# A graph network on one core: degrees written transposed and the scaled adjacency stored graph by graph

## The chip, the cores and the metric

The kernel runs on one core of a Trainium2 chip, in fp32 throughout. The metric is the device time of one execution in microseconds (us), as the median of three runs. A profiled execution is a fourth one; its trace gives the durations that are used below.

## The reference

There are 128 graphs with 128 nodes each and 512 features per node. Two residual layers follow each other, each closed by a layer norm over the features:

```python
# layer 0
deg = jnp.sum(adj, axis=-1, keepdims=True)
agg = jnp.einsum('bij,bjf->bif', adj, x) / jnp.maximum(deg, EPS)
cat = jnp.concatenate([x, agg], axis=2)
out = jnp.einsum('bnf,of->bno', cat, W)          # W: 512 x 1024
x = _layernorm(x + jax.nn.relu(out))
# layer 1: three times adj @ (x @ W_k) + b_k, relu after the first two
support = jnp.einsum('bnf,fh->bnh', x, W)
return jnp.einsum('bnm,bmh->bnh', adj, support) + b
...
x = _layernorm(x + layer_1)
```

What matters here is the division by the degree: the row of the adjacency that belongs to node i of a graph is divided by that row's sum.

## The kernel before, in words

The graphs are worked on in 32 groups of four, called quads (`NG` = 32, `G` = 4), numbered q = 0 to 31 in the code; "the sixth quad" is q = 5. All products run on TensorE. The large weight products use a seven-product scheme for blocks of two by two; after the first one or two quads it is nested, and then the operand of one such product is a 128x128 block (line 617) where the first quads use 128x256 (line 599). Prepared combinations of the first layer's weights lie in DRAM (`forms`) and are streamed into buffers named `ring` and `big`.

The division by the degree is done on the adjacency, not on the result. For a quad this goes through these steps:

- `load_adj` (line 543) loads the adjacency rows into `ar`, of which there is one buffer (every DMA of the kernel is recorded by a helper at line 320).
- `degrees` (line 550) sums each row on VectorE (line 554, `deg<-ar`), takes the maximum with a small number (line 555) and the reciprocal (line 556). The result `deg` is a tile of 128 partitions by 4: partition i holds the factors of node i of the four graphs. There are two `deg` buffers.
- One DMA writes `deg` to `dd` in DRAM (two buffers), with 16 bytes in a row for each node. A second DMA reads all 512 numbers of `dd` back into every one of the 128 partitions of `ah` (one buffer).
- `normalized` (line 563) multiplies `ah` by the transposed adjacency `at` on VectorE (line 327, `ah<-at,ah`). The order of the 512 numbers in a partition of `ah` is node first, graph second: the factors of one graph stand four floats, that is 16 bytes, apart. `at` is stored graph by graph.
- `seg_agg` (line 907) runs, for each graph g, a matmul with `AH_T[:, :, g]` as the weights (the operand that is loaded into the array ahead of the product) and 512 columns of `row` as the moving operand (line 916). In fp32 each such matmul becomes two weight loads and two passes in the trace, so that the four graphs of a quad give eight of each.

The order of the work is made in two steps. A list written out by hand (`ORDER`, `AFTER`) says in which order the stages of the quads are recorded; stage `D` is the loading of the adjacency and its degrees. Then a planner (`Plan.order`) replays all recorded operations with its own costs, its due times and the dependencies through named buffers, and emits each engine's instructions in the order in which the replay started them. It may give a GpSimd addition to VectorE (`other`) when it is late. An engine then works through its instructions strictly in that order, and SyncE's DMA queue as well: a DMA whose buffer isn't free holds back every DMA behind it. The buffer names that order `degrees` are `ar`, `deg`, `dd` and `ah`: a write to `dd` waits until the read of the same buffer into `ah` has landed.

Of the kernel before, what the change touches and what calls it, by code (L numbers as in the profile page):

```python
# [9 lines left out]
F32 = mybir.dt.float32  # L10
AF = mybir.ActivationFunctionType
OP = mybir.AluOpType
AX = mybir.AxisListType

P = 128
G = 4
# [227 lines left out]
def gnn_resnorm_kernel(  # L244
# [15 lines left out]
    nc = tc.nc  # L260
# [6 lines left out]
    dram = ctx.enter_context(tc.tile_pool(name="dram", bufs=1, space=bass.MemoryType.DRAM))  # L267
# [6 lines left out]
    def tile_of(shape, name):  # L274
        return sbuf.tile(shape, F32, tag=name, name=name)
# [8 lines left out]
    U_T = [tile_of([P, 4, 2, H], f"u{i}") for i in range(2)]  # L284
    AR_T = tile_of([P, G, P], "ar")
    AT_T = [tile_of([P, G, P], f"at{i}") for i in range(2)]
    AH_T = tile_of([P, P, G], "ah")
    ND = 8
    DEG_T = [tile_of([P, G], f"deg{i}") for i in range(2)]
    DD_T = [dram.tile([P, G], F32, tag=f"dd{i}", name=f"dd{i}") for i in range(2)]  # L290
    FORMS = dram.tile([7, P, 7, 2, P], F32, tag="forms", name="forms")
    ST_T = [tile_of([P, 6], f"st{i}") for i in range(ND)]
    END_ST = tile_of([P, 2, 2, 6], "end_st")
# [15 lines left out]
    def pinned(ins):  # L309
        return tc.keep_in_program_order(ins)  # L310

    def vector(n, emit, reads, writes, shared=False, lead=None):
        plan.op("DVE", 0.06 + 0.00123 * n, emit, reads, writes, shared, lead=lead)

    def scalar(n, emit, reads, writes, columns=0, lead=None):
        plan.op("ACT", 0.165 + 0.00083 * n + 0.1 * columns, emit, reads, writes, lead=lead)

    def dma(dst, src, reads, writes, size, queue="SP", lead=None):
        eng = nc.sync if queue == "SP" else nc.scalar
        plan.op(queue, 0.06, lambda: pinned(eng.dma_start(dst(), src())), reads, writes, size=size, lead=lead)  # L320

    def const(v):
        return lambda: v

    def add(eng, n, dst, a, b, reads, writes, op=OP.add, shared=False, lead=None):

        on_vector = lambda: pinned(nc.vector.tensor_tensor(dst(), a(), b(), op=op))  # L327
        if eng == "POOL":
            on_gpsimd = lambda: pinned(nc.gpsimd.tensor_tensor(dst(), a(), b(), op=op))  # L329
            plan.op("POOL", 0.03 + 0.00243 * n, on_gpsimd, reads, writes, True, other=(0.06 + 0.00123 * n, on_vector), lead=lead)  # L330
        else:
            vector(n, on_vector, reads, writes, shared)
# [195 lines left out]
    def at(q):  # L528
        return AT_T[q % 2], [("at", q % 2)]
# [16 lines left out]
    def load_adj_t(q):  # L546
        t, k = at(q)
        dma(const(t), const(adjT[q]), (), k, P * F * 4)

    def degrees(q):  # L550
        d, kd = DEG_T[q % 2], [("deg", q % 2)]
        dd = DD_T[q % 2]
        queue = "ACT" if q == 0 else "SP"
        vector(512, lambda: pinned(nc.vector.tensor_reduce(d, AR_T, axis=AX.X, op=OP.add)), ["ar"], kd)
        vector(90, lambda: pinned(nc.vector.tensor_scalar(d, d, DEG_EPS, None, op0=OP.max)), kd, kd, True)
        vector(90, lambda: pinned(nc.vector.reciprocal(d, d)), kd, kd)
        dma(const(dd), const(d), kd, [("dd", q % 2)], 400000 if q else 800000, queue)
        dma(
            const(AH_T), const(bass.AP(tensor=dd.tensor, offset=dd.offset, ap=[[0, P], [G, P], [1, G]])),
            [("dd", q % 2)], ["ah", "row of degrees"], 400000, queue,  # L560
        )

    def normalized(q):
        t, k = at(q)
        ah = AH_T.rearrange("p i g -> p g i")
        add("DVE", 512, const(ah), const(t), const(ah), k + ["ah"], ["ah"], OP.mult, True)

    def bank_ap(s):
        return BANK[s.index]
# [253 lines left out]
    def layernorm(i, ap, keys, of=None):  # L823

        i %= ND
        mv, rs = MV_T[i], RS_T[i]
        src, ksrc = of or (ap, keys)
        for j in range(2):
            st = ST_T[(2 * i + j) % ND]
            ks = [("st", (2 * i + j) % ND)]  # L830
            vector(512, lambda j=j, st=st: pinned(nc.vector.bn_stats(st, src(j))), ksrc(j), ks)
            vector(98, lambda j=j, st=st: pinned(nc.vector.bn_aggr(mv[:, j, :], st)), ks, [("mv", i, j)])
        kr, kb = factors(i, range(2))
        for j in range(2):
            r, b = rs[:, 0, j : j + 1], rs[:, 1, j : j + 1]
            scalar(
                512,
                lambda j=j, r=r, b=b: pinned(nc.scalar.activation(ap(j), src(j), AF.Identity, bias=b, scale=r)),
                kr + kb + ksrc(j), keys(j), columns=2,
            )  # L840
# [51 lines left out]
    def l0(q):  # L892
        return row(q, "y"), u_of(q)

    def seg_l0(q, part):
        y, u = l0(q)
        if part == 0:
            normalized(q)
        if q < EARLY:
            name, w, t = ("y", WB, y) if part < 2 else ("l0", WA, u)  # L900
            yield from (rows_b if part % 2 else rows_a)((name, q), xa(q), w, t)
        elif part < 2:
            yield from joint_a(q, xa(q), WBA, (y, u), part)
        else:
            yield from joint_b(q, xa(q), WBA, (y, u), part - 2)

    def seg_agg(q, m):
        y, u = l0(q)
        for g in (2 * m, 2 * m + 1):
            p, r = Slot("bank", seeded=True), Slot("s", spare=3)  # L910
            dma(lambda r=r: S_T[r.index].rearrange("p a b -> p (a b)"), const(x[q][:, g]), (), [r], P * F * 4, lead=LEADS[1])
            scalar(512, lambda g=g, p=p: pinned(nc.scalar.copy(bank_ap(p), u.graph(g))), u.keys((g,)), [p], lead=LEADS[0])
            plan.op(
                "PE", 0.858,
                lambda g=g, p=p: pinned(
                    nc.tensor.matmul(bank_ap(p), AH_T[:, :, g], y.graph(g), start=False, stop=True, skip_group_check=True)  # L916
                ),
                ["ah"] + y.keys((g,)), [p],
            )
            vector(  # L920
                512,
                lambda g=g, p=p, r=r: pinned(
                    nc.vector.scalar_tensor_tensor(
                        u.graph(g), bank_ap(p), 0.0, S_T[r.index], op0=OP.max, op1=OP.add
                    )
                ),
                [p, r], u.keys((g,)),
            )
            yield
        layernorm(4 * q + m, lambda j: u.graph(2 * m + j), lambda j: u.keys((2 * m + j,)))  # L930
# [317 lines left out]
    WB.sums()  # L1248
    load_adj(0)
    degrees(0)  # L1250
    load_adj_t(0)
    WA = Weight("wa", w0T[0:F])
# [21 lines left out]
    def load_degrees(q):  # L1274
        load_adj(q)
        degrees(q)
        yield

    def load_at(q):
# [4 lines left out]
        "X": load_x, "D": load_degrees, "AT": load_at,  # L1284
        **{f"L{i}": lambda q, i=i: seg_l0(q, i) for i in range(4)},
        **{f"A{i}": lambda q, i=i: seg_agg(q, i) for i in range(2)},
        **{f"G{i}": lambda q, i=i: seg_g1(q, i) for i in range(4)},
        "Ha": seg_h1_a, "Hb": seg_h1_b, "Sa": seg_s2_a, "Sb": seg_s2_b, "H2": seg_h2, "Ta": seg_s3_a, "Tb": seg_s3_b,
# [48 lines left out]
    for t in range(NG + max((lag for _, lag in tokens), default=0)):  # L1337
        for n, lag in tokens:
            q = t - lag
# [57 lines left out]
```

## Time and profile before

| | before |
|---|---|
| median of three runs | 2249.04 us (2248.91 to 2249.4) |
| the profiled execution's own time | 2250.41 us |
| its span, from the first to the last instruction | 2248.5 us |
| TensorE (PE) busy | 2235.7 us, 13,624 passes and as many weight loads |
| VectorE (DVE) busy | 1534.5 us |
| ScalarE (ACT) busy | 1330.8 us |
| GpSimd (POOL) busy | 1168.4 us |
| granted TensorE clock | 0.999 |
| DMA packets | 206,330 |
| one quad in the steady state | 69.4 us of PE |

The span of the profiled execution is 1.9 us shorter than its time, and its time is 1.4 us above the median of the timed runs. In the profile a group of instructions has its line, engine, operation, the names of what it writes and reads without buffer numbers, its shape and its count; behind the bar stand the busy time in us and the mean duration of one in ns. "PE" rows are passes of matmuls, "PEld" rows are weight loads, which run while the pass before them is still streaming. Durations of pipelined passes overlap, so a busy PE row is less than count times mean.

### The profile page before, as it was taken

How to read it: one execution, taken by the hardware profiler on the slowest of the kernel's cores; microseconds unless marked ns; L12 is line 12 of the kernel's file. 1: busy time of each engine (PE TensorE's matmuls, PEld its weight loads, DVE VectorE, ACT ScalarE, POOL GpSimd, SP SyncE). 2: the span in 40 equal slices, each digit the busy share in tenths (PEclk: the TensorE clock that was granted, in tenths of full speed). 3: DMA queues.
4: the chain of work that ended last, by engine and by line, in shares of the span. 5: the costliest groups of instructions: out<-in, count | busy, mean ns of one | idle time of the engine just before them, and what ended most of it. 6: DMA issues, size and time to landing. Idle time of an engine off the chain costs nothing.

```text
span 2248.5 us, 39986 instructions
## 1 busy us (share of the span) xinstructions
PE 2235.7 (99%) x13624; PEld 1997.9 (89%) x13624; DVE 1534.5 (68%) x3384; ACT 1330.8 (59%) x2619; POOL 1168.4 (52%) x1508
## 2 busy tenths in 40 slices
PE   8999999999999999999999999999999999999998
PEld 7888889898898888998888989889898898888997
DVE  4766667666777667677666766667666777667674
ACT  2456656566565665566665656656566556665565
POOL 0245654556645465554565455654546655455540
PEclk9999999999999999999999999999999999999999
DMA  8453445534455444454444553445534455443431
GB/s 268 125 156 125 149 142 174 175 121 145 130 176 176 127 146 134 159 176 140 139 144 143 178 162 124 147 142 172 176 121 149 129 168 176 124 141 129 153 125 38
DMA packets 206330, 333.14 MB, mean 148 GB/s; under 512 B 27056, under 2 KB 72112, under 8 KB 206128
## 3 DMA queue, kind: packets, MB, share of 16 engines
q1 hardware_dynamic: 205696, 330.19, 46.1%
q8 instruction: 109, 1.79, 0.3%
q14 instruction: 93, 0.76, 0.1%
q10 hardware_dynamic: 432, 0.40, 0.1%
HBM read 290.46 MB, written 40.04 MB: 147 GB/s over the span
## 4 chain that ended last, share of the span: by engine, by line
PE 99%; DVE 0%; DMA 0%; issue 0%; SPq 0%; DVEq 0%; ACT 0%
PE bank L617 57%; PE bank L599 21%; PE bank L916 5%; PE bank L941 5%; PE bank L1029 5%; PE bank L1216 5%; DMA big<-in_w0T_dram 0%; DVE big L327 0%; PE bank L1148 0%; SPq L320 0%; DVE ah L327 0%; DVE end_st L1153 0%; DVEq L1392 0%; DVE bank L327 0%; DVE T L327 0%
## 5 line engine op out<-in xcount | busy, mean ns | idle before, releaser
L579 ACT COPY s<-bank 128x384 f32<-128x384 f32 (+1 forms) x567 | 306.6, 541 | 320.6 <-PE bank L617 172.3
L599 PE MATMUL bank<-T,w 128*128 128x256 f32 x1792 | 416.9, 379 | 0.0
L599 PEld LDWEIGHTS bank<-T,w 128*128 128x128 f32 x1792 | 333.5, 190 | 67.2 <-issue 28.7
L329 POOL TENSOR_TENSOR T<-T 128x512 f32<-128x512 f32 (+2 forms) x295 | 279.8, 971 | 199.6 <-DVE T L327 113.2
L327 DVE TENSOR_TENSOR v<-bank,s 128x512 f32<-128x512 f32 x240 | 164.3, 684 | 205.1 <-PE bank L617 204.3
L617 PE MATMUL bank<-big,ti 128*128 128x128 f32 (+1 forms) x1470 | 274.2, 320 | 0.0
L329 POOL TENSOR_TENSOR xT<-xT 128x512 f32<-128x512 f32 (+1 forms) x244 | 237.9, 975 | 36.0 <-DVE ti L327 23.6
L585 ACT COPY bank<-bank 128x512 f32<-128x512 f32 (+2 forms) x273 | 144.0, 527 | 180.0 <-PE bank L617 153.4
L617 PEld LDWEIGHTS bank<-big,ti 128*128 128x128 f32 x1470 | 218.4, 191 | 23.8 <-issue 4.3
L617 PEld LDWEIGHTS bank<-w,T 128*128 128x128 f32 x1680 | 218.3, 192 | 17.1 <-issue 7.2
L327 DVE TENSOR_TENSOR T<-T 128x512 f32<-128x512 f32 (+1 forms) x325 | 223.9, 713 | 8.8 <-ACT T L952 5.8
L617 PEld LDWEIGHTS bank<-w,ti 128*128 128x128 f32 x1680 | 216.1, 192 | 15.5 <-issue 7.2
L617 PE MATMUL bank<-w,T 128*128 128x128 f32 x1680 | 226.5, 275 | 0.0
L617 PE MATMUL bank<-w,ti 128*128 128x128 f32 x1680 | 226.5, 275 | 0.0
L617 PE MATMUL bank<-big,T 128*128 128x128 f32 x1680 | 226.4, 275 | 0.0
L617 PEld LDWEIGHTS bank<-big,T 128*128 128x128 f32 x1680 | 218.3, 192 | 7.7
L327 DVE TENSOR_TENSOR row<-bank,s 128x384 f32<-128x384 f32 (+2 forms) x254 | 119.0, 468 | 152.3 <-PE bank L617 124.8
L617 PE MATMUL bank<-ring,xT 128*128 128x256 f32 x840 | 216.7, 380 | 0.0
L617 PE MATMUL bank<-big,xT 128*128 128x256 f32 x840 | 216.7, 379 | 0.0
L329 POOL TENSOR_TENSOR v<-v 128x384 f32<-128x384 f32 (+1 forms) x61 | 69.3, 1136 | 278.9 <-DVE v L327 144.4
L327 DVE TENSOR_TENSOR v<-v 128x512 f32<-128x512 f32 (+1 forms) x299 | 190.7, 645 | 5.3 <-DVE T L327 0.3
L329 POOL TENSOR_TENSOR s<-s,v 128x256 f32<-128x256 f32 (+1 forms) x60 | 51.8, 863 | 255.2 <-ACT bank L1210 140.7
(99 smaller groups left out, 4166.1 us busy)
## 6 DMA issues: line engine op xcount, KB each, us to landing
big<-forms SPq DMA_DIRECT2D x315, 256.0 KB, 3.2
ring<-forms SPq DMA_DIRECT2D x315, 256.0 KB, 3.3
s<-in_x_dram SPq DMA_DIRECT2D x128, 256.0 KB, 5.9
out_dram<-s SPq DMA_DIRECT2D x126, 256.0 KB, 4.0
xT<-in_xT_dram SPq DMA_DIRECT2D x62, 512.0 KB, 5.6
big<-forms SPq DMA_DIRECT2D x105, 128.0 KB, 2.7
ring<-forms SPq DMA_DIRECT2D x105, 128.0 KB, 2.8
ar<-in_adj_dram SPq DMA_DIRECT2D x32, 256.0 KB, 2.6
```

Source lines behind the costliest of these rows:

```text
L327: on_vector = lambda: pinned(nc.vector.tensor_tensor(dst(), a(), b(), op=op))
L329: on_gpsimd = lambda: pinned(nc.gpsimd.tensor_tensor(dst(), a(), b(), op=op))
L579: scalar(n * P, lambda: pinned(nc.scalar.copy(quarters_of(s, n), quarters(p, n))), [p], [s])
L585: scalar(n * P, lambda: pinned(nc.scalar.copy(quarters(s, n), quarters(p, n))), [p], [s])
L599: nc.tensor.matmul(bank_ap(p)[:, o, :], lhsT, rhs, start=start and o == 0 and c == 0, stop=c == 1, skip_group_check=True,)
L617: nc.tensor.matmul(dst, ta(), tb(), start=start and n == 0, stop=True, skip_group_check=True)
L916: nc.tensor.matmul(bank_ap(p), AH_T[:, :, g], y.graph(g), start=False, stop=True, skip_group_check=True)
L941: nc.tensor.matmul(bank_ap(p)[:, c // 2, (c % 2) * P : (c % 2 + 1) * P], u.chunk(g, c), a[:, g, :], start=c == 0, stop=True, skip_group_ch ...
L1029: nc.tensor.matmul(bank_ap(p)[:, g // 2, (g % 2) * P : (g % 2 + 1) * P], s.chunk(g, o), a[:, g, :], start=g == 0, stop=True, skip_group_ch ...
L1216: nc.tensor.matmul(bank_ap(p), a[:, g, :], s.graph(g), start=False, stop=True, skip_group_check=True)
```

## The change

From the sixth quad on (`by_graph`), the factors are written to DRAM graph by graph: the element of node i and graph g goes to place g*128 + i instead of i*4 + g. Neighbours in a partition of `deg` are then no neighbours in `dd`, and the write consists of single 4-byte pieces. The read into every partition of `ah` takes the 512 numbers in the order in which they lie, as before, so `ah` is now stored graph by graph, and both the multiplication with `at` and the weight operand of line 916 (`ah(q)[:, g]`) run over neighbouring floats. The first five quads keep the old order. `deg` and `dd` get four buffers each instead of two, in all quads.

```diff
-    AH_T = tile_of([P, P, G], "ah")
+    AH_T = tile_of([P, G * P], "ah")
     ND = 8
-    DEG_T = [tile_of([P, G], f"deg{i}") for i in range(2)]
-    DD_T = [dram.tile([P, G], F32, tag=f"dd{i}", name=f"dd{i}") for i in range(2)]
+    DEG_T = [tile_of([P, G], f"deg{i}") for i in range(4)]
+    DD_T = [dram.tile([G * P], F32, tag=f"dd{i}", name=f"dd{i}") for i in range(4)]
...
+    def by_graph(q):
+        return q >= 5
+
     def degrees(q):
-        d, kd = DEG_T[q % 2], [("deg", q % 2)]
-        dd = DD_T[q % 2]
+        d, kd = DEG_T[q % 4], [("deg", q % 4)]
+        dd = DD_T[q % 4]
...
-        dma(const(dd), const(d), kd, [("dd", q % 2)], 400000 if q else 800000, queue)
+        to = dd.rearrange("(g i) -> i g", g=G) if by_graph(q) else dd.rearrange("(i g) -> i g", g=G)
+        dma(const(to), const(d), kd, [("dd", q % 4)], 400000 if q else 800000, queue)
         dma(
-            const(AH_T), const(bass.AP(tensor=dd.tensor, offset=dd.offset, ap=[[0, P], [G, P], [1, G]])),
-            [("dd", q % 2)], ["ah", "row of degrees"], 400000, queue,
+            const(AH_T), const(bass.AP(tensor=dd.tensor, offset=dd.offset, ap=[[0, P], [1, G * P]])),
+            [("dd", q % 4)], ["ah", "row of degrees"], 400000, queue,
         )
+
+    def ah(q):
+        return AH_T.rearrange("p (g i) -> p g i" if by_graph(q) else "p (i g) -> p g i", g=G)
 
     def normalized(q):
         t, k = at(q)
-        ah = AH_T.rearrange("p i g -> p g i")
-        add("DVE", 512, const(ah), const(t), const(ah), k + ["ah"], ["ah"], OP.mult, True)
+        add("DVE", 512, const(ah(q)), const(t), const(ah(q)), k + ["ah"], ["ah"], OP.mult, True)
...
-                    nc.tensor.matmul(bank_ap(p), AH_T[:, :, g], y.graph(g), start=False, stop=True, skip_group_check=True)
+                    nc.tensor.matmul(bank_ap(p), ah(q)[:, g], y.graph(g), start=False, stop=True, skip_group_check=True)
```

## The prediction

> **What bounds the kernel now.** I read the page's busy times and chain first, then the waits of TensorE, then its groups with shapes apart, and last its timeline around one quad.
>
> ```profile
> PE 2235.7 (99%) x13624; PEld 1997.9 (89%) x13624; DVE 1534.5 (68%) x3384; ACT 1330.8 (59%) x2619; POOL 1168.4 (52%) x1508
> ...
> PE 99%; DVE 0%; DMA 0%; issue 0%; SPq 0%; DVEq 0%; ACT 0%
> ```
>
> These are busy time, share of the span and instructions of each engine, and the chain that ended last: TensorE (PE) is busy all the time and the chain never leaves it. Its waits (us in total, times, longest) say the same:
>
> ```profile
> PE bank L599 <- DMA big<-in_w0T_dram: 5.5, 1, 5.5
> PE bank L599 <- DVE T L327: 0.8, 1, 0.8
> PE bank L916 <- DVE ah L327: 0.2, 1, 0.2
> ```
>
> 6.5 us in total, all of it in the first quads. So a microsecond taken from any other engine is worth nothing, and the change can gain only where TensorE's own passes are longer than they need be. The groups of line 916 (weights `ah`) and of line 1216 (the same shape, weights `at`) show such a place:
>
> ```profile
> L916 PE MATMUL bank<-row,ah 128*128 128x512 f32 x256 | 128.2, 622 | 0.2 <-DVE ah L327 0.2
> L1216 PE MATMUL bank<-row,at 128*128 128x512 f32 x252 | 123.4, 592 | 0.0
> ...
> L916 PEld LDWEIGHTS bank<-row,ah 128*128 128x128 f32 x256 | 74.2, 314 | 15.7 <-DVE ah L327 0.6
> ...
> L1216 PEld LDWEIGHTS bank<-row,at 128*128 128x128 f32 x252 | 47.7, 190 | 20.1 <-issue 15.3
> ```
>
> A weight load from `ah`, whose floats stand 16 bytes apart, takes 314 ns where one from `at`, whose floats are neighbours, takes 190. The passes of line 916 are 30 ns longer in the mean. The timeline of TensorE for one quad shows which of them:
>
> ```profile
> 720.67 0.94 PE L617 MATMUL bank<-w,T 128*128 128x128 f32 x7
> 721.45 2.86 PE L916 MATMUL bank<-row,ah 128*128 128x512 f32 x6
> 724.14 1.05 PE L617 MATMUL bank<-w,ti 128*128 128x128 f32 x8
> 725.04 1.06 PE L617 MATMUL bank<-big,ti 128*128 128x128 f32 x8
> 725.93 1.14 PE L916 MATMUL bank<-row,ah 128*128 128x512 f32 x2
> 726.91 0.50 PE L617 MATMUL bank<-w,T 128*128 128x128 f32 x3
> ```
>
> The columns are start and length in us. Line 916 runs in two groups, of six passes and of two, each behind 128-column passes. The trace's starts give a step of 429 ns from one 512-column pass to the next and 112 ns from one 128-column pass to the next. A 314-ns load hides behind a 512-column pass and doesn't hide behind a 128-column one. The second group shows it alone: 726.91 - 725.93 = 0.98 us for two passes, where 2 x 0.429 = 0.858; 0.12 is over. In the first, 724.14 - 721.45 = 2.69 against 6 x 0.429 = 2.574; again 0.12. The first pass of a group lasts 712 ns and all others 592.
>
> [...] The trace has such a transfer, the loads of two bias vectors in 4-byte pieces; the landings are below.
>
> **The change part by part.** In the built program the order of the change's TensorE instructions is that of before, but for two matmuls moved behind three others in an early quad. So I price each part against an unchanged order.
>
> *Weights stored graph by graph.* 27 quads (q = 5 to 31) have two groups each, 54 in all. Each loses 712 - 592 = 120 ns, but not wholly: twice near the end line 1216, with its contiguous weights, follows a 128-column pass, and there the step is 432 instead of 429 ns. That leaves 3 ns, so 117.5 ns a group: 54 x 117.5 = 6.35 us, all on the chain. The check from the group's means: (622 - 592) x 256 = 7.7 us over 32 quads, 6.5 over 27. Bounds: 0, if the load is slow for another reason than the step, and 6.5.
>
> *The multiplication on VectorE.* Today:
>
> ```profile
> L327 DVE TENSOR_TENSOR ah<-at,ah 128x512 f32<-128x512 f32 x32 | 38.1, 1189 | 39.3 <-DMA at<-in_adjT_dram 39.3
> ```
>
> The same operation between contiguous tiles takes 685 ns (`v<-v`) to 845 (`T<-T`). I take 700, so about 27 x 0.49 = 13 us of VectorE. It is worth nothing: at 753.6 us the product is made for passes that begin 37 us later. If that cover were gone, it would be 0.49 us a quad.
>
> *The write in 4-byte pieces.* 27 writes of 512 pieces instead of 128, 27 x 384 = 10,368 packets more. The issue on SyncE's queue goes from 320 ns (`dd<-deg`) to the 378 of the bias loads, 27 x 0.06 = 1.6 us of that queue. The landing now is 1.6 us; the bias loads took 5.0 to 5.9 beside the traffic of the start, so I take 3 and keep 1.6 to 6. Nobody waits for it soon: with four buffers the write of quad q+4 stands behind the read of quad q, so it is four quads, 277 us, ahead of its reader. Queued behind it on SyncE are a form load of 256 KB (issue to first use 26.8 us, landing 3.2), the next `ar` and `at`. Its cover is 23 us. Cost: nothing.
>
> *Four buffers.* In the steady state the SyncE queue holds the same list a quad, and the wait before `dd<-deg` stays, since that is for the read just issued:
>
> ```profile
> SPq L320 <- DMA ah<-dd: 80.4, 28, 3.5
> ```
>
> What moves lies in the fill. Stage D of the next four quads (each a 256-KB `ar` load, a row sum, a maximum, a reciprocal; two of their `dd` writes) comes forward into the stretch from 115 to 150 us, among form loads on SyncE. VectorE gives 4 x 1.0 us there (0.68, 0.16 and 0.18 for the three) and is 64% busy in that stretch (22.57 of 35 us). Each extra `ar` waits for the row sum before it. By the trace's starts the form loads up to 146 us have 8.2 us or more from issue to first use (13.6 at 120.5 us), so they can be late by 5 us without harm. From 148 us on it is 3.3 to 8.6; the tightest are two of 128 KB at 152.6 and 158.7 us with 3.3, which land in about 2.7. By its place in the queue the last extra `ar` goes out at about 149.5 us and, at 2.6 us a landing, is in before 152.6. I take 0, and keep 0 to 3 us of loss. At the other end the last eight quads have no stage D instead of the last four; there the planner hands two more `T` sums a quad to VectorE (8 in all). The last four quads run so already, at 69.4 us a quad as in the middle, so that costs nothing.
>
> *Sum.* -6.35 us. The span of the profiled execution would go from 2248.5 to 2242.15, its time from 2250.41 to 2244.1. The median of before is 1.4 us below that time; I subtract from the median: 2249.04 - 6.35 = 2242.7.
>
> **Rivals.** *The load stays slow or stays hidden* (the change doesn't do what it says): if the array were fed by something other than the step, all else is off the chain, and the time is 2249.0. Against it stands 190 ns of every load from contiguous tiles.
>
> *Part of the gain is given back in the fill:* a form load comes late behind the extra `ar` loads, once or several times. For it: SyncE's queue is strict, and the two loads above have 0.6 us to spare. Two delays of 1 to 1.5 us make about 2245.5.
>
> *Slower:* the extra `ar` loads stall SyncE itself. They wait for row sums on VectorE, which wait for what stands before them there; such waits now last up to 3.9 us. It takes from TensorE once a wait exceeds the 5 us that the form loads behind can lose, and it ends slower by more than 0.2% once the four take 10.9 us together. With 9 us each: 4 x 4 = 16 us, so 2249.04 - 6.35 + 16 = 2258.7. Against it: the sums stand where VectorE has gaps of 1 to 4 us.
>
> *Slower by the pieces:* the 4-byte write blocks the queue for over 23 us in each quad, four times what the bias loads took; 24 us would give 27 - 6 = 21 us of loss. I count this as nearly excluded.
>
> **How the numbers follow.** The forecast gets 0.80, its own range being 2241.9 to 2244.3 (the bounds of 3 ns, a microsecond or so in the fill, and the scatter of the runs, 0.5 us). The gain given back 0.09, no effect 0.06, slower 0.05 for both forms. To hold 8 in 10 with a margin, the range runs from 2241.6 to 2245.6, which takes in most of the gain given back. 0.2% of 2249 is 4.5 us, about what can be told from no change; the line is 2244.5. Faster by more: the forecast and a quarter of the second case, 0.83. Same: the rest of it and no effect, 0.12. Slower 0.05.
>
> **What would show it.** Right: weight loads of line 916 with a median near 190 ns; its passes with a mean near 597 (five quads keep 622) and no first pass of 712 after 370 us; a quad of 69.15 us instead of 69.38; `ah<-at,ah` near 700; packets near 216,700; no new wait of TensorE. Wrong: loads still at 309; a wait of TensorE on `big`, `ring` or `ah` between 110 and 170 us; `dd<-deg` landing after 20 us.

## The result and the profile after

| | before | after |
|---|---|---|
| median, 22 runs each | 2249.35 us | 2253.39 us |
| ratio after/before, 95% interval | | 1.0015 (1.001 to 1.0021) |
| profiled execution: time / span | 2250.41 / 2248.5 us | 2254.32 / 2252.5 us |

The change makes the kernel slower: the median is 4.0 us higher, and the ratio gives 0.15%, or 3.4 us (2.2 to 4.7). I had forecast 6.35 us faster. The lines of the new kernel stand six further down from line 565 on: 916 is now 922, 617 is 623, 554 is 557.

The page of the changed kernel, busy times and chain:

```profile
PE 2232.2 (99%) x13624; PEld 1973.4 (88%) x13624; DVE 1535.5 (68%) x3391; ACT 1330.3 (59%) x2619; POOL 1159.9 (51%) x1501
...
PE 97%; DMA 2%; DVE 0%; ACT 0%; issue 0%; SPq 0%; DVEq 0%
PE bank L623 57%; PE bank L605 21%; PE bank L1035 5%; PE bank L922 5%; PE bank L947 5%; PE bank L1222 5%; DMA ar<-in_adj_dram 1%; DMA dd<-deg 0%; DMA big<-in_w0T_dram 0%; DMA ah<-dd 0%; DVE deg L557 0%; ACT bank L879 0%; DVE big L327 0%; DVE T L327 0%; PE bank L1154 0%
```

TensorE has 3.5 us less to do, and yet the span is 4 us longer. The chain now leaves TensorE for 2% of the span, to DMAs, the loads of `ar` above all.

The gain itself is there. Groups of TensorE and its weight loads, then its timeline in the same quad that the prediction showed:

```profile
L922 PE MATMUL bank<-row,ah 128*128 128x512 f32 x256 | 121.8, 598 | 0.1
...
L922 PEld LDWEIGHTS bank<-row,ah 128*128 128x128 f32 x256 | 48.5, 210 | 28.6 <-issue 19.4 <-ACT bank L918 6.5 <-DVE ah L327 0.5
```

```profile
730.16 2.74 PE L922 MATMUL bank<-row,ah 128*128 128x512 f32 x6
732.73 1.05 PE L623 MATMUL bank<-w,ti 128*128 128x128 f32 x8
733.62 1.06 PE L623 MATMUL bank<-big,ti 128*128 128x128 f32 x8
734.52 1.02 PE L922 MATMUL bank<-row,ah 128*128 128x512 f32 x2
735.38 0.83 PE L623 MATMUL bank<-w,T 128*128 128x128 f32 x6
```

The six passes take 732.73 - 730.16 = 2.57 us instead of 2.69, the two 0.86 instead of 0.98. In the trace the first step of such a group is 431 or 432 ns from the sixth quad on, where it was 550. That is the 117.5 ns of the prediction, 54 times. A quad takes 69.15 us, as forecast.

What was lost lies in the fill. TensorE's waits and its timeline around the longest one:

```profile
PE bank L605 <- DMA big<-in_w0T_dram: 5.7, 1, 5.7
PE bank L623 <- ACT v L651: 5.4, 1, 5.4
PE bank L623 <- DVE row L327: 1.3, 1, 1.3
PE bank L605 <- DVE T L327: 0.8, 1, 0.8
```

```profile
133.38 0.38 PE L623 MATMUL bank<-w,T 128*128 128x128 f32 x2
139.20 1.62 PE L623 MATMUL bank<-w,T 128*128 128x128 f32 x6 [5.43 <-ACT v L651]
140.62 1.91 PE L623 MATMUL bank<-big,xT 128*128 128x256 f32 x4
```

Two waits are new, of 5.4 and 1.3 us. After the first one four 256-column passes take 1.91 us where they take 1.03: the clock has dropped, to a granted 0.50 from 139.2 to 143.3 us. The stretch around the wait shows it too; the columns are its length, PE, PEld, DVE, ACT and POOL busy, then the granted clock, the DMA share and GB/s. In the 20 us before, the clock was 1.00.

```profile
130.00:150.00 20.00, 14.56 (x79) 13.09 (x78) 12.35 (x29) 9.91 (x21) 7.13 (x10) 0.83 0.64 191
```

The chain tells who kept TensorE waiting. The start of each piece and its length are in us; pieces of `issue` of 0.02 to 0.04 us are left out, and more of ScalarE's work where the dots stand:

```profile
115.30 11.21 DMA ar<-in_adj_dram
126.53 0.70 DVE deg L557
127.25 8.15 DMA ar<-in_adj_dram
135.41 0.69 DVE deg L557
136.10 0.09 DVE mv L874
136.21 0.82 ACT bank L879 x2
...
138.70 0.48 ACT v L651
139.20 21.23 PE bank L623 x134
```

Two `ar` loads take 11.2 and 8.2 us. Before, such a load took 2.6 us in the median, and the write of the factors 1.6:

```profile
ar<-in_adj_dram SPq DMA_DIRECT2D x32, 256.0 KB, 2.6
...
dd<-deg SPq DMA_DIRECT2D x31, 2.0 KB, 1.6
```

VectorE's row sum waits for each of the two loads. Behind the second row sum stands a small operation of the layer norm (line 874); ScalarE waits for that, and behind it on ScalarE stands the copy that frees a bank for TensorE. The queue of SyncE shows what went out just ahead of these loads:

```profile
114.73 0.37 SPq L320 DMA_DIRECT2D dd<-deg  x1
115.30 0.35 SPq L320 DMA_DIRECT2D ar<-in_adj_dram  x1
120.38 0.32 SPq L320 DMA_DIRECT2D big<-forms  x1
120.79 0.39 SPq L320 DMA_DIRECT2D dd<-deg  x1
```

The two `dd<-deg` are the writes of quads 5 and 6, the first ones in 4-byte pieces. In the list of DMAs, with median us to landing at the end, `dd<-deg` went from 1.6 to:

```profile
dd<-deg SPq DMA_DIRECT2D x31, 2.0 KB, 10.4
```

(The median is over the five landings that the trace could match; three are of writes in pieces: 12.1, 11.6 and 10.4, the first of them the write of 120.79 us.) The trace's packets say where the time isn't spent: the 512 packets of 4 bytes of the first write all start between 115.0 and 116.0 us, at 7 ns each. Only then do the 2-KB packets behind them crawl, for ten microseconds: 256 of them start between 116.3 and 126.8 us.

The second wait has another way. These are waits of VectorE, with us in total, times and the longest:

```profile
DVE deg L557 <- DMA dd<-deg: 13.4, 17, 3.2
DVE deg L557 <- DMA ar<-in_adj_dram: 11.4, 2, 6.1
```

The second line is the chain above. In the first, the row sum of quad q+4 writes the `deg` buffer that the write of quad q still reads, and so it waits until that write has landed. At 194.5 us the wait, for the write of 183.36 us, reached TensorE through an operation of VectorE that stood behind the row sum (the 1.3 us at `row`). The others of these waits were covered.

The loss by the trace's steps between passes: 5.6 us for the wait at 133 us, 2.1 for the passes at a granted clock of 0.50 after it, 1.55 for the wait at 194 us, 0.7 for smaller ones (0.26 at 128 us, 0.45 around 435 us), together 10.0. Less the gain of 6.35 that is 3.6, against 4.0 between the medians and 3.4 by the ratio.

### The profile page after: what moved, and what is told of

Its sections match the earlier page's. It is cut to its first block, busy times and chain, and to the rows that moved or that the text cites. A ratio compares the mean times of both kernels' runs of the same rounds, so it can differ in the third digit from the quotient of the medians.

```text
span 2252.5 us, 39981 instructions
## 1 busy us (share of the span) xinstructions
PE 2232.2 (99%) x13624; PEld 1973.4 (88%) x13624; DVE 1535.5 (68%) x3391; ACT 1330.3 (59%) x2619; POOL 1159.9 (51%) x1501
## 2 busy tenths in 40 slices
DMA packets 216699, 333.15 MB, mean 148 GB/s; under 512 B 37424, under 2 KB 82480, under 8 KB 216496
## 4 chain that ended last, share of the span: by engine, by line
PE 97%; DMA 2%; DVE 0%; ACT 0%; issue 0%; SPq 0%; DVEq 0%
PE bank L623 57%; PE bank L605 21%; PE bank L1035 5%; PE bank L922 5%; PE bank L947 5%; PE bank L1222 5%; DMA ar<-in_adj_dram 1%; DMA dd<-deg 0%; DMA big<-in_w0T_dram 0%; DMA ah<-dd 0%; DVE deg L557 0%; ACT bank L879 0%; DVE big L327 0%; DVE T L327 0%; PE bank L1154 0%
## 5 line engine op out<-in xcount | busy, mean ns | idle before, releaser
L329 POOL TENSOR_TENSOR T<-T 128x256 f32<-128x256 f32 (+2 forms) x287 | 269.7, 961 | 207.0 <-DVE T L327 114.3
L623 PEld LDWEIGHTS bank<-big,ti 128*128 128x128 f32 x1470 | 218.3, 191 | 24.4 <-issue 4.7
L329 POOL TENSOR_TENSOR s<-s,v 128x384 f32<-128x384 f32 (+1 forms) x61 | 52.8, 865 | 250.2 <-ACT bank L1216 130.5
```

The source lines that it names most:

```text
L623: nc.tensor.matmul(dst, ta(), tb(), start=start and n == 0, stop=True, skip_group_check=True)
```

## The experiments

Theory A, from the traces: a write in 4-byte pieces is slow and holds up the loads issued after it; in the fill VectorE waits for such a load with a layer norm queued behind. Rival B: moving four stages D into the fill costs the time, whatever the pieces. All ratios are against runs of the kernel before on the same chip; us are worked out from the ratio and its median.

**Four buffers alone** (and the new layout in no quad):

```diff
-        return q >= 5
+        return False
```

> Four buffers for deg and dd in all quads, but every quad keeps the old order and writes 16 bytes a node; the instruction order is that of the changed kernel. Theory A (the writes in 4-byte pieces land after 10 to 12 us, hold up the adjacency load that is issued behind them in the fill, and VectorE waits for it with the layer norm queued behind): adjacency loads between 110 and 160 us land in about 3 us, no wait of TensorE at 133 us, time 2249 to 2250. Rival B (moving four stages D into the fill costs the time, whatever the size of the pieces): the wait of 5.4 us at 133 us stays, about 2259 (9.9 us of loss, none of the gain).

Measured: 2250.66 against 2250.36 us, ratio 1.0000 (0.9992 to 1.0008). No new wait of TensorE; the `ar` load at 113.4 us, behind the write of quad 5, lands in 4.0 us:

```profile
DMA to landing us min/median/max: 4.0/4.0/4.0
```

B falls: with the same instruction order as the changed kernel and 16-byte pieces no loss can be told (the interval leaves room for 1.8 us, and B asked for 9.9).

**The layout with two buffers:**

```diff
-    DEG_T = [tile_of([P, G], f"deg{i}") for i in range(4)]
-    DD_T = [dram.tile([G * P], F32, tag=f"dd{i}", name=f"dd{i}") for i in range(4)]
+    DEG_T = [tile_of([P, G], f"deg{i}") for i in range(2)]
+    DD_T = [dram.tile([G * P], F32, tag=f"dd{i}", name=f"dd{i}") for i in range(2)]
```

(and `q % 4` to `q % 2`).

> The layout from the sixth quad on as in the change, but two buffers for deg and dd as before; the instruction order is that of the kernel before. Theory A: the first write in pieces goes out at about 176 us, no adjacency load stands close behind it in the fill, so no wait at 133 us; the row sum that reuses deg may wait a few us for the landing. 2243 to 2245. Rival B: stage D stays where it was, 2243. If the pieces cost time in the steady state as well, 27 times a little: 2246 or more.

Measured: 2243.72 against 2250.36 us, ratio 0.9969 (0.9957 to 0.9981), so 7.0 us faster (4.3 to 9.7). The gain arrives once no `ar` load of the fill stands close behind a write in pieces. The pieces show in the steady state too. With two buffers it is the row sum of quad q+2 that waits for the landing of the write that still reads its `deg` buffer:

```profile
  DMA dd<-deg: 23.9, 24
```

Those are 24 waits of about 1 us, and one of them reaches TensorE (pieces of `issue` are left out):

```profile
450.69 12.46 DMA dd<-deg
463.17 0.04 DVE deg L557
463.77 1.02 DVE row L327 x2
464.84 1.13 PE bank L1222 x2
```

That costs 0.7 us of wait. The others are covered.

**The layout from the ninth quad on**, with four buffers:

```diff
-        return q >= 5
+        return q >= 8
```

> The change with the new layout from the ninth quad on (q >= 8) instead of the sixth; four buffers, and the instruction order of the changed kernel. Only the writes of quads 5, 6 and 7 go back to 16 bytes a node. Theory A: the waits at 133 us and 194 us are gone, 24 quads gain 0.235 us each = 5.6 us, 2243.7. Rival B: the waits stay, about 2254.

Measured: 2245.95 against 2250.36 us, ratio 0.9978 (0.997 to 0.9987), 5.0 us faster (2.9 to 6.8). The waits at 133 and 194 us are gone. TensorE has two new waits of together 1.8 us, at 812 and 1297 us, each behind a row sum that waited for the landing of a write (VectorE has 19 such waits, 24.4 us in total); the forecast gain of 5.6 us lies inside the interval. B would have had 2254.

**The layout in quads 5 and 6 only**, with four buffers:

```diff
-        return q >= 5
+        return q in (5, 6)
```

> The change with the new layout in quads 5 and 6 alone; four buffers, and the instruction order of the changed kernel. Theory A: the two writes in pieces of the fill are there, so the wait of 5.4 us at 133 us and the slow passes after it stay, the wait at 194 us (behind the write of quad 7) goes; gain of two quads 0.5 us, loss about 8: 2256.5 to 2257.5. Rival B: the same 2258 to 2259, with the wait at 194 us as well. A time near 2249 would show that neither two writes nor the move make the loss.

Measured: 2260.76 against 2250.36 us, ratio 1.0042 (1.003 to 1.0055), 9.5 us slower (6.8 to 12.4). Two writes are enough for a loss as large as that of the whole change: the wait at 134 us is there (6.0 us), that at 194 us is not. I had forecast a loss of about 7.5 us, which lies inside the interval; the wait was somewhat longer than 5.4 us in this run, and the slow passes after it (again 1.91 us for four of 256 columns) cost 2.0 us, much as before.

**The two writes on ScalarE's queue.** Is it the order in the queue, or something that all queues share?

```diff
+        wq = "ACT" if q in (0, 5, 6) else "SP"
...
-        dma(const(to), const(d), kd, [("dd", q % 4)], 400000 if q else 800000, queue)
+        dma(const(to), const(d), kd, [("dd", q % 4)], 400000 if q else 800000, wq)
```

> The change with the two writes in pieces of the fill (quads 5 and 6) issued from ScalarE's DMA queue instead of SyncE's; all other DMAs as in the change. The planner moves a few instructions of the fill with it. Theory A1 (an adjacency load waits behind the pieces of its own queue): the loads issued next to those writes land in 3 to 5 us, no wait of TensorE of several us at 133 us, 2244 to 2246. Theory A2 (the pieces hold the DMA engines, or the memory, for every queue): such a load lands in about 11 us again, the wait stays, 2252 to 2256.

Measured: 2253.75 against 2250.08 us, ratio 1.0015 (1.0009 to 1.0022). The write went out on ScalarE's queue at 114.51 us, the load on SyncE's at 115.1; this is that load and who waited for it:

```profile
L320 SPq DMA_DIRECT2D ar<-in_adj_dram x1: 333/333/333, 115.1 to 115.1; - x1
...
  DVE deg L558: 6.1, 1
...
DMA to landing us min/median/max: 11.2/11.2/11.2
```

It is the same 11.2 us. TensorE waited 7.9 us, now for `T` (8.7 with a second wait); the planner had moved a few other instructions along with the writes. So it isn't the order within one queue that makes the load late, and another queue doesn't help.

**Pieces of 8 bytes.** Two graphs stay neighbours, 256 pieces a write, weights with a step of 8 bytes:

```diff
-        to = dd.rearrange("(g i) -> i g", g=G) if by_graph(q) else dd.rearrange("(i g) -> i g", g=G)
+        to = dd.rearrange("(h i b) -> i h b", h=2, b=2) if by_graph(q) else dd.rearrange("(i g) -> i g", g=G)
```

(the source `d` is viewed in pairs as well, and `ah` is read as `p (h i b) -> p h b i`).

> The change with two graphs kept next to each other: from the sixth quad on the factors go out in 256 pieces of 8 bytes a quad instead of 512 of 4, and the weights of a graph stand 8 bytes apart; four buffers, and the order of the changed kernel. Theory A (the landing follows the number of pieces): the write lands in 5 to 6 us, the adjacency load behind it in about 6, so the wait of 5.4 us at 133 us shrinks below 1; 2244 to 2246 if the weight load at a step of 8 bytes takes 190 ns[...]. If that load takes 309 ns, nothing is gained on the passes: 2250 to 2251. If the landing goes by the bytes and not by the pieces, the wait stays: 2253.

Measured: 2245.38 against 2250.08 us, ratio 0.9977 (0.9967 to 0.9987), 5.2 us faster (2.9 to 7.4). The write at 114.7 us lands in 3.6 us and the `ar` load behind it in 5.2; there is no new wait of TensorE. Half as many pieces were to land in 5 to 6 us, half the time of the 4-byte write, and they took less than that: the landing is not simply proportional to the number of pieces. The weight loads of one quad:

```profile
L930 PEld LDWEIGHTS bank<-row,ah x8: 195/197/198, 720.9 to 725.4; 128*128 128x128 f32 x8
```

197 ns instead of 309 at 16 bytes and 190 for neighbours: a step of 8 bytes is nearly free, at 7 ns. Why a step of 16 bytes costs more is not shown.

**VectorE makes the order.** The DMAs stay as before, with two buffers; the multiplication reads the old order and writes graph by graph into a tile of its own, in all quads:

```diff
+    AG_T = tile_of([P, G, P], "ag")
...
-        add("DVE", 512, const(ah), const(t), const(ah), k + ["ah"], ["ah"], OP.mult, True)
+        add("DVE", 512, const(AG_T), const(t), const(ah), k + ["ah"], ["ah"], OP.mult, True)
...
-                    nc.tensor.matmul(bank_ap(p), AH_T[:, :, g], y.graph(g), start=False, stop=True, skip_group_check=True)
+                    nc.tensor.matmul(bank_ap(p), AG_T[:, g], y.graph(g), start=False, stop=True, skip_group_check=True)
```

> The kernel before with one more tile of 128 x 512 floats: VectorE's multiplication reads ah in the old order and writes the product graph by graph into the new tile, which line 916 takes its weights from, in all 32 quads. The DMAs, the two buffers and the instruction order are those of before. Theory A: the weight loads take 190 ns, 62 groups gain 117.5 ns each = 7.3 us; the multiplication stays near 1.2 us, its read being still strided, off the chain; dd lands in 1.6 us and no row sum waits. 2242 to 2243, and below the two-buffer form of the change by 0.5 to 2 us. If the gain of the change came from VectorE's shorter multiplication, nothing is gained: 2249.

Measured: 2241.97 against 2250.08 us, ratio 0.9967 (0.9955 to 0.9979), 7.4 us faster (4.7 to 10.1). It is 0.33% below the kernel before; the changed kernel stands 0.15% above it. The form with two buffers (0.31% below) can't be told from this one: the 0.5 to 2 us that I expected between them are not shown.

```profile
L917 PEld LDWEIGHTS bank<-row,ag 128*128 128x128 f32 x256 | 43.8, 191 | 30.8 <-issue 22.7 <-ACT bank L913 7.4 <-DVE ag L328 0.6
...
L328 DVE TENSOR_TENSOR ag<-at,ah 128x512 f32<-128x512 f32 x32 | 38.0, 1187 | 37.7 <-DMA at<-in_adjT_dram 37.7
```

All weight loads are fast, and VectorE's multiplication is as slow as before (1187 ns). So the gain comes from the loads, and the strided read on VectorE costs TensorE nothing.

**One more write that nobody reads.** The kernel of the first experiment (old layout everywhere, four buffers) with an extra write of the factors in 4-byte pieces to a scratch buffer in quads 5 and 6, once without gaps and once with the pieces 512 bytes apart:

```diff
+    SCR = [dram.tile([G * P], F32, tag=f"scr{i}", name=f"scr{i}") for i in range(2)]
...
+            if q in (5, 6):
+                pinned(nc.sync.dma_start(SCR[q % 2].rearrange("(g i) -> i g", g=G), d))
```

```diff
-    SCR = [dram.tile([G * P], F32, tag=f"scr{i}", name=f"scr{i}") for i in range(2)]
+    SCR = [dram.tile([G * P, P], F32, tag=f"scr{i}", name=f"scr{i}") for i in range(2)]
...
-                pinned(nc.sync.dma_start(SCR[q % 2].rearrange("(g i) -> i g", g=G), d))
+                pinned(nc.sync.dma_start(SCR[q % 2][:, 0].rearrange("(g i) -> i g", g=G), d))
```

> The four-buffer kernel with the old order everywhere, and in quads 5 and 6 one more write of the factors, in 512 pieces of 4 bytes to a scratch buffer that nobody reads, laid out as in the change (2 KB without gaps), issued just ahead of the ordinary 16-byte write. If the pieces alone make the loss: the adjacency loads behind them land in about 11 us, TensorE waits 5 to 6 us at 133 us, about 2259 to 2261 as with the layout in quads 5 and 6 alone. If reading the new layout has a part in it: near 2250.

Measured without gaps: 2260.57 against 2250.75 us, ratio 1.0045 (1.003 to 1.006), 10.1 us slower. TensorE waits 5.5 us on the copy `v`, as in the changed kernel. The two scratch writes in the list of DMAs, and the landing of the `ar` load behind the first:

```profile
scr<-deg SPq DMA_DIRECT2D x2, 2.0 KB, 11.4
...
DMA to landing us min/median/max: 11.3/11.3/11.3
```

> The same with the pieces of the scratch write 512 bytes apart. Theory P1 (what costs is the number of small writes to DRAM): the adjacency loads land in about 11 us and the wait stays, 2259 to 2261. Theory P2 (what costs is that many pieces of different partitions fall into the same short stretch of memory[...]): the loads land in 3 to 5 us, no wait, 2250.

Measured with gaps: 2250.50 against 2250.75 us, ratio 1.0000 (0.9991 to 1.0009), no wait of TensorE above 1.1 us after the start. The same lines:

```profile
scr<-deg SPq DMA_DIRECT2D x2, 2.0 KB, 2.7
...
DMA to landing us min/median/max: 4.3/4.3/4.3
```

The `ar` load lands in 11.3 us without gaps and in 4.3 with them. As many pieces of the same size came from the same tile, so neither their number nor their size alone is what is slow: it takes that they lie together in 2 KB of DRAM, without gaps.

## Why the prediction was wrong, point by point

- *What bounds the kernel, and the gain on the passes:* right. 117.5 ns a group and 54 groups were forecast; the steps of 550 ns became 431 or 432. The mean of the passes (598 for 597), the weight loads (191 ns in the quad shown) and the packets (216,699 for 216,700) came as said. The versions with 8-byte pieces and with VectorE making the order, the latter with the DMAs of before, gained 5.2 (2.9 to 7.4) and 7.4 us (4.7 to 10.1), which agrees with the forecast for their 54 and 62 groups.
- *The multiplication on VectorE:* right that it is worth nothing; it took 793 ns in the median for 700, and the version that leaves it slow gains as much as any.
- *The write in 4-byte pieces:* **this step failed.** I took a landing of 3 us and kept 1.6 to 6, from the loads of two bias vectors in 4-byte pieces. They are reads of DRAM, and took 5.0 to 5.9 us; a write of 512 such pieces side by side took 9.0 to 14.1 us wherever the trace could match its landing. Worse than the size was the "Cost: nothing" that I drew from it. I did not ask what else slows down while the write lands: I listed the `ar` load among what is queued behind it, and gave it its undisturbed 2.6 us. It took 11.2, whichever queue the write was on. And "nobody waits for it soon" looked only at the reader of `dd`. The row sum that next writes the same `deg` buffer waits as well, 17 times in the changed kernel, and one of these waits cost TensorE 1.55 us.
- *Four buffers:* "I take 0, and keep 0 to 3 us of loss". By themselves they cost nothing that could be told (ratio 1.0000), as said. But they bring the writes of quads 5 and 6 into the fill, next to `ar` loads that VectorE needs at once. With two buffers those writes lie elsewhere, and 7.0 us are gained. The loss needs both halves of the change, and I had priced each alone. The 22.57 us that I gave for VectorE in the stretch from 115 to 150 us are those of 120 to 155; from 115 to 150 it was 21.05, and nothing hung on it.
- *The slower rival:* its place was right, its chain wasn't. I had SyncE stalled on row sums and form loads late. In fact the row sums waited for the loads (6.1 and 5.3 us), and the way to TensorE led through VectorE's order: the layer norm's small operations behind the row sum. None of the signs of being wrong that I had named came up: the weight loads were fast, TensorE's new waits were not on `big`, `ring` or `ah`, and no `dd<-deg` that the traces could match took over 14.1 us. And after the 5.4 us of wait the granted clock was 0.50 until 143.3 us: passes of 256 columns step by 427 ns instead of 216, 2.1 us more of loss that I had not counted for any wait.

Still open: why neighbouring pieces are slow. The pieces with gaps are as small, 4 bytes, and land in 2.7 us, against 11.4 without gaps, so their size alone is not it. The pieces with gaps also cover 256 KB of DRAM instead of 2, so being neighbours and being crowded into one place are not told apart, and it was not tried how far apart the pieces must be; 512 bytes was the only distance. The 8-byte pieces halved the number of pieces and, with it, how many lie in the same 2 KB, so they don't help here either.

## What to carry to other kernels

Before a step is written off as hidden, ask what its transfer does to every other transfer in flight, not only who waits for it: an in-order engine that waits for a late load holds all that is queued behind it (VectorE waited 6.1 and 5.3 us for two loads here, and TensorE 5.4 us for what stood behind them). Ask also which buffer the transfer still reads, and who writes that buffer next. Don't scatter single floats into neighbouring places of DRAM close ahead of loads that are needed at once (such a load took 11.2 us instead of 2.6); away from them the same writes left a gain of 7.0 us here. If the engine that touches the data anyway has the slack, it can write them in the order in which the next one reads. And where a weight load follows a short pass (of 128 columns here), look at the step of its elements: 16 bytes made a load 119 ns longer here, 8 bytes 7.

## What the runs showed of the hardware that was not expected

- Writes of `deg` to DRAM from the sixth quad on, 2 KB each, without gaps: 1.4 to 3.6 us in pieces of 16 bytes (median 1.5), 2.8 to 4.7 in pieces of 8 (median 3.6), 9.0 to 14.1 in pieces of 4. In pieces of 4 with 512 bytes from one to the next: 1.8 and 3.6.
- Behind such a write in 4-byte pieces a 256-KB load of other data landed in 11.2 us, and just as late when the write went out on another engine's queue, though the write's own packets had all started within 1 us.
- After an idle stretch of 5.4 us on TensorE the granted clock was 0.50 from 139.2 to 143.3 us, which cost another 2.1 us.
